# Gate logits as eight extra columns of the local attention's products, and expert rows in 68 tiles of 256 and 15 of 128 rows

## The chip, the cores and the metric

The kernel runs on one core of one Trainium2 chip, in one launch. The metric is the device time of one execution in microseconds (us), as the median of several runs. All arithmetic is in fp32, apart from a few bf16 constants.

## The reference

A batch of 16 images with 128 rows of text each becomes 16 sequences of 569 rows of 256 features. Three residual parts follow, and then a recurrent one. Cut to what matters here:

```python
h = concatenate([tokens(x), txt], axis=1)            # convolution and attention over 441 positions
h = h + attn(layernorm(h))                           # windows of 64 rows, 8 heads, out @ w_out.T + b_out
xf = layernorm(h).reshape(-1, 256)
logits = xf @ gate_w + gate_b                        # gate_w: 256 x 8
probs = softmax(logits)
top2_vals, top2_idx = top_k(probs, 2)                # two of the eight experts for each row
for e in range(8):                                   # 256 -> 512 -> 256, gelu between
    out += cw[:, e:e+1] * (gelu(xf @ w1[e] + b1[e]) @ w2[e] + b2[e])
h = h + out
h = h + layer1_attn(layernorm(h))                    # a cumulative sum over time
h = h + layer1_lstm(layernorm(h))                    # an LSTM over the 569 steps
```

The kernel runs an expert only on the rows that picked it. The logits of a row need the row after the attention's output projection and after its normalisation.

## The kernel before, in words

The rows are kept as 8 pairs of sequences (`NP`) with 9 chunks of 128 rows each (`NC`), 72 chunks in all. The work has three stages, one after the other.

**The first stage** makes the tokens, the window attention and the choice of experts. Several Python generators describe it: `features` and `projections` (convolution, queries and values), `tokens` (attention of the tokenizer), `norms` (the normalisation before the window attention), four copies of `windows` (one chunk each: `wtr` transposes, `wqk` queries and keys, `wsc` scores, `wv` values, `wpt` and `wav` the weighted sum, `wob` the output projection L777), `sent_rows` (the normalisation after it, into the tile `XN`), and `routing`. A planner, the class `Order`, replays the generators against a cost that each gives for its next instruction, and writes one fixed order of instructions for each engine. Every engine then works through its list in order. On GpSimd (POOL) the planner's `"POOL+"` and on VectorE (DVE) its `"DVE+"` steps are kept from running at the same time.

`routing` works on the nine chunks of a pair (the last pair in parts of 4, 3 and 2 chunks). For each group of up to four chunks it transposes the normalised rows (`rtr`, L800), copies them out of PSUM (`rxT`, L804), multiplies them by the gate's weights, padded to 32 columns so that four chunks lie side by side in the array (`lg`, L810), copies the result (`lgs`, L816), transposes it back (`lt`, L819) and adds the bias (L821). The softmax, the rank of each expert and the place of each row follow on DVE. `send` then scatters each chunk twice into the DRAM tensor `XS` with an indirect DMA from POOL (L908), so that the rows of one expert lie together.

**The second stage** runs the experts (`experts`). The rows of every expert are cut into tiles of 256 rows. Since each expert's last tile is only partly full, 79 tiles are provided for 18432 row places (2 experts for each of 9216 rows). A few small DVE instructions work out from the counts which expert and which first row each tile has (`need`, `where`, L1120 to L1149). SyncE (SP) reads these numbers into registers and issues for each tile the load of its expert's weights (`w`, 1154 KB, L1168) and of its rows (`xs`, L1174), into five buffers each. Four generators `tiles(slot)` take the tiles in turn. A tile is four transposes (`xtr`, L1212), eight products with the first weights (`hp`, L1241), four gelus on ScalarE (ACT, L1248), eight products with the second weights (`y`, L1255), a bias add on DVE (L1261), and two indirect DMAs back to the tensor `YT` (L1184). An fp32 product shows up as two records, each a weight load (PEld) and a pass (PE).

**The third stage** runs layer 1: `fronts`, `backs` and the LSTM's steps, in the order of a second planner.

Of the kernel before, what the change touches and what calls it, by code (L numbers as in the profile page):

```python
# [35 lines left out]
    ("bk1", 2), ("bq1", 2), ("bk2", 1), ("bq2", 1), ("ln_w", 2), ("ln_b", 2),  # L36
# [28 lines left out]
TILES = [(2 * 8 * 128 * len(g) + E * (TILE - 1)) // TILE for g in GROUPS]  # L65
# [229 lines left out]
def kernel(ctx: ExitStack, tc: tile.TileContext, a: dict, out: bass.AP):  # L295
# [63 lines left out]
    gw = route.tile([128, 2, 32], F32, name="gw")  # L359
# [16 lines left out]
    H, XN, made = {}, {}, []  # L376
# [12 lines left out]
    def rows_of(p, c):  # L389

        while len(made) >= ROWS:
            before = ("normed", *made[len(made) - ROWS])
            if before in first.events:
                break
            yield "at", before
        made.append((p, c))
        H[p, c] = hp.tile([128, D], F32, name=f"h{p}_{c}", tag="h", bufs=ROWS)
        return H[p, c]

    def texts():  # L400

        for p in range(NP):
            if p:
                yield "at", ("token", p - 1, 3)
            for c in (7, 6, 8):
                h = yield from rows_of(p, c)
                if c == 8:
                    yield "POOL", 0.3
                    nc.gpsimd.memset(h, 0.0)
                lo, hi, at = {6: (25, 64, 0), 7: (0, 64, 39), 8: (0, 25, 103)}[c]  # L410
                for s in range(2):
                    nc.sync.dma_start(
                        h[64 * s + lo : 64 * s + hi], a["txt"][2 * p + s][at : at + hi - lo, :]
                    )
            first.mark(("text", p), 8.0)

    def setup():
# [12 lines left out]
        nc.scalar.dma_start(wout, a["w_out"].rearrange("(k p) n -> p k n", p=128))  # L430
# [8 lines left out]
        nc.gpsimd.memset(gw, 0.0)  # L439
        nc.scalar.dma_start(gw[:, :, :E], a["gate_w"].rearrange("(k p) n -> p k n", p=128))  # L440
# [42 lines left out]
        for i, (name, w, b, to) in enumerate((("bv", wo, "bo", tok_b), ("vb", wout, "b_out", win_b))):  # L483
            v = tmp.tile([128, 2, 128], F32, name=f"{name}_every")
            for k in range(2):
                nc.vector.tensor_copy(v[:, k, :], col(name, k).to_broadcast([128, 128]))
            mm = place_of(f"{name}_row", 2 + i)
            for k in range(2):
                nc.tensor.matmul(mm[:, :D], v[:, k, :], w[:, k, :], start=(k == 0), stop=(k == 1))
            nc.vector.tensor_tensor(to, mm[:, :D], row(b), ALU.add)  # L490
# [77 lines left out]
    def tokens(slot):  # L568

        last = NIMG - 384  # L570
        for n in range(slot, 7 * NP, 2):
# [46 lines left out]
            for q, i in to:  # L618
                yield "DVE", 0.48
                nc.vector.scalar_tensor_tensor(  # L620
                    H[p, i][q], mm[q], share_[q], tok_b[q], ALU.mult, ALU.add
# [3 lines left out]
    def norm(h, to, name, slot):  # L625
# [3 lines left out]
        nc.vector.bn_stats(st, h)  # L629
# [4 lines left out]
        yield "POOL", 0.85  # L634
        nc.gpsimd.tensor_scalar(rstd, mv[:, 1:2], EPS, None, ALU.add)
        nc.gpsimd.tensor_tensor(rstd, rstd, mhalf[:, :1], ALU.pow)
        yield "DVE+", 0.5
        nc.vector.tensor_scalar(to, h, mv[:, 0:1], rstd, ALU.subtract, ALU.mult)
# [12 lines left out]
    def sent_rows(p, c, h, slot):  # L651

        if p not in XN:
            if p > 1:
                yield "at", ("sent", p - 2)
            if p not in XN:
                XN[p] = xnp.tile([128, NC, WIDE], F32, name=f"XN{p}", tag="XN", bufs=2)
                yield "POOL", 0.2
                nc.gpsimd.tensor_copy(XN[p][:, :, D], cols[:, COL["row"] + NC * p : COL["row"] + NC * (p + 1)])
        yield from norm(h, XN[p][:, c, :D], f"r{p}_{c}", slot)  # L660
# [11 lines left out]
    def windows(slot):  # L672

        kb, vb = KB[slot], VB[slot]
        for n in range(slot, NC * NP, WINDOWS):
# [28 lines left out]
            nc.gpsimd.tensor_tensor(h, h, win_b, ALU.add)  # L704
# [16 lines left out]
            v = place_of(f"wv{u}", slot)[:, :D].rearrange("p (w n) -> p w n", w=2)  # L721
            for w in range(2):
                for k in range(2):
                    yield "PE", 0.22, "64"
                    for odd in range(2):
# [4 lines left out]
                        )  # L730
            top = wk.tile([128, NH], F32, name=f"wtop{u}", tag=f"wtop{slot}", bufs=1)
            yield "DVE", 0.68
            nc.vector.tensor_reduce(top, S, AX.X, ALU.max)
            for odd in range(2):
# [39 lines left out]
            ob = place_of(f"wob{u}", slot)[:, :D]  # L774
            for m in range(2):
                yield "PE", D * COLUMN
                nc.tensor.matmul(ob, AT[:, m, :], wout[:, m, :], start=(m == 0), stop=(m == 1))  # L777
            yield "DVE", 0.42
            nc.vector.tensor_tensor(h, ob, h, ALU.add)
            nc.sync.dma_start(HD[p][:, c, :], h)  # L780
# [4 lines left out]
    def routing():  # L785

        for p, lo, hi in PARTS:
            u, n = f"{p}_{lo}", hi - lo
            pr = wk.tile([128, n, E], F32, name=f"pr{u}", tag="pr", bufs=1)
            for g0 in range(lo, hi, 4):  # L790
                m = min(4, hi - g0)
                xT = wk.tile([128, 2, 4, 128], F32, name=f"rxT{p}_{g0}", tag="rxT", bufs=1)
                for c0 in range(g0, g0 + m, 2):
                    two = min(2, hi - c0)
                    tr = place_of(f"rtr{p}_{c0}", 7).rearrange("p (k c n) -> p k c n", k=2, c=2)
                    for c in range(c0, c0 + two):
                        yield "at", ("normed", p, c)
                        for k in range(2):
                            yield "PE", TURN
                            nc.tensor.transpose(  # L800
                                tr[:, k, c - c0, :], XN[p][:, c, 128 * k : 128 * k + 128], ident
                            )
                    yield "ACT", 0.6
                    nc.scalar.copy(xT[:, :, c0 - g0 : c0 - g0 + two, :], tr[:, :, :two, :])  # L804

                lg = place_of(f"lg{p}_{g0}", 7)
                for k in range(2):
                    yield "PE", 0.24, "32"
                    for j in range(m):
                        nc.tensor.matmul(  # L810
                            lg[32 * j : 32 * j + 32, :128], gw[:, k, :], xT[:, k, j, :],
                            start=(k == 0), stop=(k == 1),
                        )
# [1262 lines left out]
```

## Time and profile before

The profiled execution took 3360.87 us itself; its span, in which the tables below are, is 3359.0 us.

| | |
|---|---|
| time before, median of 3 runs | 3378.91 us (3378.6 to 3380.3) |
| profiled execution, own time / span | 3360.87 / 3359.0 us |
| PE, weight loads, DVE, ACT, POOL busy | 3055.1, 2231.5, 2027.2, 1471.9, 786.6 us |
| mean granted TensorE clock | 0.978 |
| first stage, to the first expert product | 0 to 978 us |
| second stage, to the last `y` product's start | 978 to 1573 us |
| third stage | 1573 to 3359 us |

An engine's busy time is the union of its instructions' durations. A product's record is longer than its share of a sequence of products, since they are pipelined: what a product costs in a sequence is read as the length of the sequence divided by its number. A line of groups gives busy time and mean duration after the bar, and then the idle time of the engine just ahead of the group with what ended it.

### The profile page before, as it was taken

How to read it: one execution, taken by the hardware profiler on the slowest of the kernel's cores; microseconds unless marked ns; L12 is line 12 of the kernel's file. 1: busy time of each engine (PE TensorE's matmuls, PEld its weight loads, DVE VectorE, ACT ScalarE, POOL GpSimd, SP SyncE). 2: the span in 40 equal slices, each digit the busy share in tenths (PEclk: the TensorE clock that was granted, in tenths of full speed). 3: DMA queues.
4: the chain of work that ended last, by engine and by line, in shares of the span. 5: the costliest groups of instructions: out<-in, count | busy, mean ns of one | idle time of the engine just before them, and what ended most of it. 6: DMA issues, size and time to landing. Idle time of an engine off the chain costs nothing.

```text
span 3359.0 us, 134328 instructions
## 1 busy us (share of the span) xinstructions
PE 3055.1 (91%) x57536; PEld 2231.5 (66%) x57536; DVE 2027.2 (60%) x6787; ACT 1471.9 (44%) x5030; POOL 786.6 (23%) x1524
## 2 busy tenths in 40 slices
PE   5999999999859999997899999999999999999884
PEld 3666666666548888886566676766666666666652
DVE  4677777766732222222566777777777777766555
ACT  3545545454412222221444555555555555554442
POOL 1243554445533322232311001010101010100000
PEclk9999999999979999998999999999999999999997
DMA  5111221111176666664333333333333333333333
GB/s 180 53 46 57 89 79 54 55 38 41 42 251 234 220 231 225 225 229 141 100 100 88 90 82 86 84 94 78 97 77 92 84 93 79 76 91 80 90 103 113
DMA packets 276070, 366.81 MB, mean 109 GB/s; under 512 B 144480, under 2 KB 220176, under 8 KB 263312
## 3 DMA queue, kind: packets, MB, share of 16 engines
q1 hardware_dynamic: 249360, 300.91, 30.5%
q0 software_dynamic: 14496, 39.75, 3.1%
q10 hardware_dynamic: 11616, 17.56, 1.8%
q8 instruction: 451, 7.39, 0.9%
q14 instruction: 147, 1.20, 0.1%
HBM read 239.33 MB, written 118.75 MB: 107 GB/s over the span
## 4 chain that ended last, share of the span: by engine, by line
PE 37%; DVE 7%; ACT 5%; issue 2%; SPq 1%; DMA 1%; POOL 0%; ACTq 0%; DVEq 0%; POOLq 0%
PE gates L1741 13%; PE xm_False L1085 5%; PE out_gate L1750 2%; PE ek L1085 2%; PE po_False L1085 2%; PE z L1085 2%; PE v L1085 2%; PE eq L1085 2%; PE ds_False L1085 2%; ACT act L1762 1%; PE r_False L1085 1%; ACT th L1798 1%; DVE ab L1777 1%; DVE cT L1790 1%; DVE act L1783 1%
## 5 line engine op out<-in xcount | busy, mean ns | idle before, releaser
L1741 PE MATMUL gates<-W_hh,X 128*16 128x96 f32 (+1 forms) x18176 | 487.9, 248 | 63.9 <-DVE X L1805 61.6
L1741 PEld LDWEIGHTS gates<-W_hh,X 128*16 128x16 f32 (+1 forms) x18176 | 373.6, 103 | 258.5 <-DVE X L1805 245.0
L1248 ACT ACTIVATE hT<-hp,w 128x256 f32<-128x256 f32 x316 | 132.6, 472 | 481.5 <-PE hp L1241 314.5
L1762 ACT ACTIVATE act<-gates 128x96 f32<-128x96 f32 x568 | 142.1, 250 | 444.1 <-PE gates L1741 437.0
L1255 PE MATMUL y<-w,hT 128*128 128x256 f32 x1264 | 289.7, 382 | 5.2 <-ACT hT L1248 1.5
L1085 PE MATMUL xm_False<-W_ih,dxT_False 128*32 128x256 f32 x4352 | 292.3, 380 | 2.3 <-DVE dxT_False L1271 1.9
L1241 PE MATMUL hp<-xt,w 128*128 128x256 f32 x1264 | 287.6, 381 | 1.0 <-ACT hT L1248 1.0
L1777 DVE SCALAR_TENSOR_TENSOR ab<-act 128x64 f32<-128x64 f32 x568 | 127.9, 225 | 258.2 <-ACT act L1762 250.8
L1255 PEld LDWEIGHTS y<-w,hT 128*128 128x128 f32 x1264 | 236.8, 190 | 45.2 <-ACT hT L1248 14.4
L1684 PEld LDWEIGHTS <-nil 128*32 128x32 bf16 x4552 | 190.3, 94 | 111.0 <-issue 53.0
L1241 PEld LDWEIGHTS hp<-xt,w 128*128 128x128 f32 x1264 | 239.9, 191 | 35.7 <-ACT hT L1248 1.5
L1184 POOL DMA_INDIRECT YT<-ys,to x158 | 153.4, 971 | 440.4 <-DVE ys L1261 408.9
L1261 DVE TENSOR_TENSOR ys<-y,w 128x512 f32<-128x512 f32 x79 | 54.6, 691 | 316.3 <-PE y L1255 241.1
L1750 PE MATMUL out_gate<-W_hh,X 128*32 128x64 f32 x9088 | 233.8, 219 | 0.7 <-issue 0.7
L1690 ACT COPY gates<-xc 128x96 f32<-128x96 f32 x569 | 138.6, 244 | 182.0 <-DMA xc<-XCD 75.4
L1750 PEld LDWEIGHTS out_gate<-W_hh,X 128*32 128x32 f32 x9088 | 187.9, 110 | 2.9 <-issue 1.1
L1805 DVE SCALAR_TENSOR_TENSOR X<-toT,th 128x32 f32<-128x32 f32 x569 | 109.9, 193 | 120.5 <-ACT th L1798 116.9
L1798 ACT ACTIVATE th<-cT 128x32 f32<-128x32 f32 x569 | 130.5, 229 | 92.9 <-DVE cT L1790 43.1
L1301 POOL TENSOR_SCALAR d_False_rstd<-d_False_mv 128x2 f32<-128x2 f32 (+1 forms) x36 | 9.0, 250 | 671.8 <-DVE d_False_mv L1293 547.4
L908 POOL DMA_INDIRECT XS<-XN,at x144 | 149.1, 1035 | 45.6 <-issue 24.6
L693 PE MATMUL wqk<-wxT,wqkv 128*128 128x128 f32 x1152 | 150.6, 278 | 8.9 <-ACT wxT L687 8.6
L693 PEld LDWEIGHTS wqk<-wxT,wqkv 128*128 128x128 f32 x1152 | 139.4, 192 | 24.9 <-ACT wxT L687 13.5
(356 smaller groups left out, 6497.9 us busy)
## 6 DMA issues: line engine op xcount, KB each, us to landing
w<-in_wpack SPq DMA_DIRECT2D x79, 1154.0 KB
taps<-in_taps SPq DMA_DIRECT2D x16, 1764.0 KB
xc<-XCD SPq DMA_DIRECT2D x71, 384.0 KB
XCD<-xp_False SPq DMA_DIRECT2D x256, 96.0 KB
xs<-XS SPq DMA_DIRECT2D x79, 258.0 KB
yg<-YT SPq DMA_DIRECT2D x72, 256.0 KB
HD<-h SPq DMA_DIRECT2D x72, 128.0 KB
fh<-HD SPq DMA_DIRECT2D x72, 128.0 KB
```

What stands on the lines that cost most here:

```text
L693: nc.tensor.matmul(qk[:, j, m, :], wqkv[:, k, D * j + 128 * m : D * j + 128 * m + 128], xT[:, k, :], start=(k == 0), stop=(k == 1),)
L908: fill(0, nc.gpsimd.indirect_dma_start(out=XS[0], out_offset=bass.IndirectOffsetOnAxis(ap=at[:, i, c - lo : c - lo + 1], axis=0), in_=XN[p ...
L1085: nc.tensor.matmul(out[own], lhsT[:, own], rhs, start=start, stop=stop)
L1184: keep(nc.gpsimd.indirect_dma_start(out=YT, out_offset=bass.IndirectOffsetOnAxis(ap=to[:, i : i + 1], axis=0), in_=ys[:, i, :], in_offset= ...
L1241: nc.tensor.matmul(hp[:, i, :], w1[:, k, hc * 128 : (hc + 1) * 128], xT[:, k, :], start=(k == 0), stop=(k == 1),)
L1255: nc.tensor.matmul(y[:, i, :], hT[:, hc, 128 * i : 128 * i + 128], w2[:, hc, :], start=(hc == 0), stop=(hc == 3),)
L1684: nc.tensor.matmul(g[32 * q : 32 * q + 32, :n], nil[:, :32], nil[:, :n], start=True, stop=last)
L1741: nc.tensor.matmul(GC[32 * q : 32 * q + NB * (1 + half), :96], before[:, kk, NB * (1 - half) :], Whh[:, kk, own : own + 96], start=False, ...
L1750: nc.tensor.matmul(GO[32 * q : 32 * q + 32, :64], before[:, kk, :], Whh[:, kk, own : own + 64], start=False, stop=(kk == 1),)
L1762: nc.scalar.activation(act[:, :96], GC[:, :96], AF.Tanh, scale=0.5), begun.pop((k, t))
L1777: nc.vector.scalar_tensor_tensor(ab, act[:, :64].rearrange("p (g x) -> p g x", g=2), 1.0, act[:, 64:].rearrange("p (g x) -> p g x", g=2), ...
L1798: nc.scalar.activation(th.rearrange("p k x -> p (k x)"), cT, AF.Tanh, scale=0.5)
```

## The change

It has two parts, which share no instruction.

**Gate logits in the window attention.** Write g for `gate_w` with the mean of each column taken off (so that the normalisation's own subtraction of a mean has no effect on it). With h2 = h + attention, the logits are `rstd2 * (h2 @ g) + gate_b`. The setup makes g (`gate_sum`), W·g with W the output projection (`wout_t`, `wout_gate`) and the bias's part, and puts W·g as columns 256 to 263 of `wout`. The rows `h` get nine more columns: eight for h2 @ g and one for sqrt(var + eps) of the first normalisation, since the product takes `xT`, the normalised rows. In each chunk four small products (64 x 8) follow the value products, a DVE instruction scales them by that ninth column, the output projection is 264 columns wide, and after the second normalisation one DVE instruction multiplies by `rstd` and adds `gate_b`, into `LG`. POOL works out the ninth column with one more `pow`. The six steps in `routing` from `rtr` to the bias add fall away.

**Tiles of two sizes.** 68 tiles of 256 rows are taken from the full 256-row pieces of the experts, and what is left of each expert goes to 15 tiles of 128 rows. The tiles are worked through in the sequence 0 to 7, then a small one after every four large ones. A small tile loads half the rows and all of its expert's weights. More DVE instructions work out the places.

```diff
-TILES = [(2 * 8 * 128 * len(g) + E * (TILE - 1)) // TILE for g in GROUPS]
+WHOLE = [(2 * 8 * 128 * len(g) - E * TILE // 2 + TILE - 1) // TILE for g in GROUPS]
+TILES = [
+    w + (2 * 8 * 128 * len(g) + E * (TILE // 2 - 1)) // (TILE // 2) - 2 * w for w, g in zip(WHOLE, GROUPS)
+]
...
-    gw = route.tile([128, 2, 32], F32, name="gw")
+    gw = route.tile([128, 2, E], F32, name="gw")
...
-        H[p, c] = hp.tile([128, D], F32, name=f"h{p}_{c}", tag="h", bufs=ROWS)
+        H[p, c] = hp.tile([128, D + E + 1], F32, name=f"h{p}_{c}", tag="h", bufs=ROWS)
...
+        mm = place_of("gate_sum", 4)
+        for k in range(2):
+            nc.tensor.matmul(mm[:, :E], ones, gw[:, k, :], start=(k == 0), stop=(k == 1))
+        for k in range(2):
+            nc.vector.scalar_tensor_tensor(
+                gw[:, k, :], mm[:, :E], -1.0 / D, gw[:, k, :], ALU.mult, ALU.add
+            )
+        for m in range(2):
+            mm = place_of(f"wout_t{m}", 5)
+            woutT = tmp.tile([128, 2, 128], F32, name=f"woutT{m}")
+            for k in range(2):
+                nc.tensor.transpose(
+                    mm[:, 128 * k : 128 * k + 128], wout[:, m, 128 * k : 128 * k + 128], ident
+                )
+            nc.scalar.copy(woutT.rearrange("p k n -> p (k n)"), mm[:, :D])
+            mm = place_of(f"wout_gate{m}", 4)
+            for k in range(2):
+                nc.tensor.matmul(mm[:, :E], woutT[:, k, :], gw[:, k, :], start=(k == 0), stop=(k == 1))
+            nc.scalar.copy(wout[:, m, D:], mm[:, :E])
...
+        over = mv[:, 1:2]
+        nc.gpsimd.tensor_scalar(over, over, EPS, None, ALU.add)
+        nc.gpsimd.tensor_tensor(rstd, over, mhalf[:, :1], ALU.pow)
+        if name[0] == "w":
+            nc.gpsimd.tensor_tensor(h[:, D + E :], over, half, ALU.pow)
...
+        rstd = yield from norm(h, XN[p][:, c, :D], f"r{p}_{c}", slot)
+        yield "DVE", 0.19
+        nc.vector.scalar_tensor_tensor(
+            LG[p][:, c, :], h[:, D : D + E], rstd, frow("gate_b", E), ALU.mult, ALU.add
+        )
...
+            for k in range(2):
+                yield "PE", 0.06, "64"
+                for w in range(2):
+                    own = slice(64 * w, 64 * w + 64)
+                    nc.tensor.matmul(
+                        vg[own, D : D + E], xT[:, k, own], gw[:, k, :], start=(k == 0), stop=(k == 1)
+                    )
...
+            yield "DVE", 0.2
+            nc.vector.scalar_tensor_tensor(
+                h[:, D : D + E], vg[:, D : D + E], h[:, D + E :], win_b[:, D:], ALU.mult, ALU.add
+            )
...
-                yield "PE", D * COLUMN
+                yield "PE", (D + E) * COLUMN
                 nc.tensor.matmul(ob, AT[:, m, :], wout[:, m, :], start=(m == 0), stop=(m == 1))
...
-            for g0 in range(lo, hi, 4):
... 
+            for c in range(lo, hi):
+                yield "at", ("normed", p, c)
+            pr = LG[p][:, lo:hi, :]
...
+        each = (whole - 2 * slots) / (NT - whole)
+        order = sorted(
+            range(NT), key=lambda j: j if j < whole else 2 * slots - 0.5 + (j - whole) * each
+        )
...
-                            yield "PE", 256 * COLUMN
+                            yield "PE", 128 * n * COLUMN
                             nc.tensor.matmul(
-                                hp[:, i, :], w1[:, k, hc * 128 : (hc + 1) * 128], xT[:, k, :],
+                                hp[:, i, : 128 * n], w1[:, k, hc * 128 : (hc + 1) * 128], xT[:, k, :],
                                 start=(k == 0), stop=(k == 1),
                             )
...
-                for i in range(2):
+                for i in range(n):
                     for hc in range(4):
                         yield "PE", 256 * COLUMN
```

In a small tile `n` is 1, in a large one 2. The fixed order of PE and of ACT in the third stage is the same in both kernels; on DVE and SP a few of its instructions change places.

## The prediction

> **What bounds the kernel now.** I read the stages' table first (busy us of each engine in six stretches of the span; then the granted clock, the DMA share and GB/s):
>
> ```profile
> 34.00:100.00 66.00, 54.32 (x356) 32.80 (x357) 41.97 (x101) 31.20 (x84) 12.04 (x22) 0.94 0.32 116
> 100.00:880.00 780.00, 729.87 (x6460) 514.47 (x6458) 553.85 (x1458) 394.46 (x1073) 352.83 (x615) 1.00 0.16 56
> 880.00:978.00 98.00, 44.63 (x405) 33.95 (x404) 56.81 (x199) 25.01 (x64) 54.78 (x98) 0.74 0.50 170
> 978.00:1573.00 595.00, 587.46 (x2815) 509.01 (x2815) 141.14 (x484) 132.57 (x316) 180.75 (x331) 1.00 0.65 220
> 1573.00:3359.00 1786.00, 1628.15 (x47476) 1133.54 (x47474) 1228.18 (x4528) 885.58 (x3487) 178.77 (x432) 0.98 0.35 90
> ```
>
> The experts (978 to 1573) are PE's alone: 587 of 595 us. From 100 to 880 PE is busy 94%, with DVE second at 71%. From 880 to 978 no engine fills its time, which is a chain. The change leaves the last stage's order on PE alone; I count 0 there.
>
> The groups of the products that the change removes (busy us, mean ns):
>
> ```profile
> L800 PE MATMUL rtr<-ident,XN 128*128 128x128 f32 x144 | 26.3, 287 | 1.3 <-DVE part L887 0.6 <-DVE XN L638 0.5
> ...
> L810 PE MATMUL lg<-rxT,gw 128*32 128x128 f32 x288 | 15.7, 283 | 0.9 <-ACT rxT L804 0.7
> ...
> L819 PE MATMUL lt<-ident,lgs 128*128 128x128 f32 (+3 forms) x24 | 7.2, 301 | 1.9 <-ACT lgs L816 1.9
> ```
>
> Last the timeline (start, length), for rates and for the chain:
>
> ```profile
> 436.60 1.86 PEld L693 LDWEIGHTS wqk<-wxT,wqkv 128*128 128x128 f32 x16 [0.17 <-ACT wq L702]
> ...
> 907.83 0.38 PEld L810 LDWEIGHTS lg<-rxT,gw 128*32 128x32 f32 x16 [0.17 <-issue]
> ...
> 908.41 0.73 PEld L777 LDWEIGHTS wob<-wout,wAT 128*128 128x128 f32 x4 [0.20 <-ACT VB L737]
> ...
> 929.49 0.55 PEld L766 LDWEIGHTS wav<-wPT,VB 128*64 128x64 f32 x16 [0.20 <-ACT wPT L759]
> ...
> 940.08 0.71 PEld L800 LDWEIGHTS rtr<-ident,XN 128*128 128x128 f32 x4 [0.65 <-PE pos L876]
> ...
> 963.40 0.91 SPq L1168 DMA_DIRECT2D w<-in_wpack  x2
> ...
> 1203.02 3.42 PEld L1255 LDWEIGHTS y<-w,hT 128*128 128x128 f32 x16
> ```
>
> Here 16 passes of 256 columns take 3.42 us (0.214 each), 16 of 128 columns 1.86 (0.116), 16 of 64 by 64 with two side by side 0.55 (0.034). A gate group of four chunks holds PE from 907.83 to the next product at 908.41: 0.58 us. SP's loads of `w` in the steady experts stand at 1201.22 and, two tiles on, at 1216.28: **7.53 us for a tile**, and 79 x 7.53 = 595.
>
> [...]
>
> **The change, part by part.**
>
> *Tiles.* Eleven large tiles go: 11 x 7.53 = 82.8 us. A small one has 16 passes of 128 columns (16 x 0.116 = 1.86), 8 of 256 (1.71) and two transposes (the group L1212: 43.1 us for 316, 0.136 each, 0.27). A large tile by this sum is 32 x 0.214 + 4 x 0.136 = 7.39, measured 7.53, so I add 0.1 for its stalls: 3.94, times 15 = 59.1. Gain **23.7**. Bounds: with passes of exactly half (0.107) 26; with passes that keep the weight load's mean record of 0.191 a tile is 5.1 and the gain 6. I take the sequence's rate, since it is the same shape.
> Four more loads of 1154 KB cost nothing while PE covers them: a round of four large tiles and one small moves 5 x 1154 + 4.5 x 514 KB = 8.3 MB in 4 x 7.53 + 3.94 = 34 us, 243 GB/s; the steady stage shows up to 237, and the DMA-bound 950 to 1000 us 277. Without cover a small tile would last as long as its 1.45 MB: 5.2 us, 19 in all lost. SP issues two register reads and two DMAs more for each of four tiles; POOL sends seven scatters fewer (0.97 us each, idle there).
> The extra planning on DVE is 3 instructions ahead of the first tiles' numbers and 16 after them, some 0.18 us each, 3.4 in all: DVE ended at 957.1, and SP's first `w` at 963.40 waited for the last scatters, so 6.3 us of cover hides it. Without that it costs 3.4.
>
> *Gate path removed.* PE: 144 transposes at 0.116 = 16.7; 24 gate groups at 0.58 = 13.9[...]; 24 transposes back at 0.14 = 3.4[...]: **38** us. The busy sums (26.3 + 15.7 + 7.2 = 49) are the upper end. ACT loses the copies L804 (21.7) and L816 (6.4), DVE L821 (4.3): neither sets the pace.
> *Added.* 72 x 8 passes of 64 by 8[...], taken as wav's 34: 19.6[...]. Eight more columns on 288 passes: 8/256 of 0.214, 1.9. DVE gets two instructions per chunk: 72 x (0.2 + 0.19) = 28 us. POOL gets 72 `pow`: the row of the same form lasts 0.62, 45 us on an engine busy 353 of 780.
> So PE wins 38 - 21.5 = 16.5[...], and less than nothing only if DVE's part below decides. The new DVE step waits for the gate product and for POOL's `pow`; behind it on DVE stand the sums that PE's `wpt` needs. DVE's net 24 us are 3% of the stretch, and PE idles there 50 us, mostly for DVE: I give back 4. Gain **12.5**.
>
> *Setup.* Convolution starts at 33.97, right after the product `vb_row`, on which it waits. Now a chain stands ahead: DVE's two corrections (0.4), then twice a product pair (0.5 as L473) and an ACT copy (0.17), one 0.37 us copy, two more DVE copies (0.35), four more small passes (0.5). **Loss 3** (1 to 5); taps arrive earlier, so nothing hides it.
>
> *Tail.* From the last chunk's transposes (940.08) to its logits (L821, ended at 943.98) 3.9 us fall away, with the order on PE (after `pos`) that held them. What is late next is POOL: 18 scatters of 1.27 us are 22.9 of the 28.8 between 927.05 and 955.86, so at most 5.9 can go from there. In the new order POOL has the last chunk's subtraction behind five scatters, 6.4 us. Gain **4** (0 to 9).
>
> Sum: 23.7 + 12.5 - 3 + 4 = 37.2. The profiled execution then has a span of 3321.8 and 3323.7 of its own; it stood 18.0 under the median of the three runs, so against that I predict 3378.9 - 37 = **3342**.
>
> **Rivals.**
> *Only the experts pay.* The small products cost 53 ns, DVE takes back the rest, the tail stays with POOL: 16.5 - 11 - 5.5 = 0, so 23.7 - 3 = 21: 3358. For it: PE's idle time ends mostly on DVE. Against: PE is at 94%.
> *A small tile is not a small tile.* Its passes stay at the weight load's length or it waits for its weights: 6 + 12.5 - 3 + 4 = 19.5: 3359. For it: a small tile loads as many weights. Against: 0.116, and five buffers.
> *DVE becomes the bound of the first stage: slower.* From 100 to 880 it is at 71%, and at 80% in single stretches of 50 us. If each of 72 chunks pays both new instructions and their two waits (0.39 + 2 x 0.25 = 0.89 us, 64), PE's gain is void, since PE's in-order list waits: 23.7 - 3 - 64 + 4.3 + 4 = -35: 3414. It decides once a chunk's net delay passes some 0.35 us (25 over 72). Against: PE's own waits for DVE are only some 25 us in this stretch.
> *The whole gate path was on the path*[...]: 33 + 23.7 - 3 + 9 = 63: 3316.
>
> **How the numbers follow.** Chances: the forecast 0.58, only the experts 0.2, tile not small 0.06, the whole path 0.08, DVE 0.08. The forecast's own range is 3327 to 3354. With the two at 3358 and 3359 it reaches up to 3363; the low end, 3322, leaves out most of the 3316 case, the high end the DVE case. Within 0.2% is 6.8 us, about what this kernel's measurement can tell from no change. Faster than that takes all but the DVE case and a bit of the second and third failing together: 0.9; slower 0.06; the same 0.04.
>
> **What would show it.** In the new profile: first small-column passes behind `wv` at about 0.03 us each; the first stage's 100 to 880 work done some 12 us sooner; convolution starting near 37; the first expert product at about 964; the SP loads of `w` five to a round of 34 us, so the experts last 571; the last stage again 1786. A round above 36 us makes the tile part wrong; a first product after 975 makes the gate part wrong; DVE as the releaser of much more PE idle time makes the third rival right.

## The result, and the profile after

| | before | after |
|---|---|---|
| time, median of 5 runs each on one chip | 3378.91 us (3378.2 to 3382.1) | 3333.89 us (3330.9 to 3342.4) |
| ratio, 95% interval | | 0.9874 (0.9858 to 0.9889) |
| profiled execution, own time / span | 3360.87 / 3359.0 us | 3333.89 / 3332.1 us |
| mean granted TensorE clock | 0.978 | 0.973 |

The change saves 45.0 us between the medians, and 27 us between the two profiled executions: the one of before stood 18.0 us under its median, the one of after at its median. Most of what follows turns on these 18 us.

The stages' table of after (busy us of PE, PEld, DVE, ACT, POOL; granted clock, DMA share, GB/s), cut where the stages now begin:

```profile
36.20:100.00 63.80, 52.78 (x376) 33.11 (x378) 39.36 (x102) 31.55 (x85) 12.50 (x22) 0.95 0.33 120
100.00:880.00 780.00, 723.99 (x6592) 510.65 (x6588) 581.70 (x1579) 371.26 (x1012) 401.79 (x705) 0.99 0.17 58
880.00:976.00 96.00, 45.97 (x372) 36.84 (x373) 57.70 (x218) 22.53 (x59) 45.84 (x81) 0.67 0.43 144
976.00:1541.00 565.00, 558.07 (x2810) 491.04 (x2809) 143.47 (x508) 132.89 (x332) 174.10 (x316) 1.00 0.69 239
1541.00:3332.10 1791.10, 1631.48 (x47476) 1130.98 (x47474) 1229.21 (x4528) 885.76 (x3487) 179.67 (x434) 0.98 0.34 90
```

Against before's rows, the experts last 565 us in place of 595, the first expert product comes at 976 in place of 978, and the last stage, whose order on PE did not change, takes 1791 in place of 1786. Read so, the experts give 30 us, and everything done to the gate gives 2.

The experts' groups by form, SP's loads of `w` in the steady experts (start, length), and PE's sequence over one small tile:

```profile
L1309 PE MATMUL hp<-xt,w 128*128 128x256 f32 x1088 | 253.4, 382 | 0.0
L1309 PE MATMUL hp<-xt,w 128*128 128x128 f32 x240 | 31.6, 275 | 0.0
```

```profile
1201.81 0.33 SPq L1230 DMA_DIRECT2D w<-in_wpack  x1
...
1208.31 0.33 SPq L1230 DMA_DIRECT2D w<-in_wpack  x1
...
1211.96 0.33 SPq L1230 DMA_DIRECT2D w<-in_wpack  x1
...
1218.72 0.33 SPq L1230 DMA_DIRECT2D w<-in_wpack  x1
...
1228.65 0.33 SPq L1230 DMA_DIRECT2D w<-in_wpack  x1
...
1235.51 0.33 SPq L1230 DMA_DIRECT2D w<-in_wpack  x1
```

```profile
1207.29 2.35 PE L1309 MATMUL hp<-xt,w 128*128 128x128 f32 x14
1209.48 1.89 PE L1323 MATMUL y<-w,hT 128*128 128x256 f32 x8
```

Five loads, one round of four large tiles and one small, take 1235.51 - 1201.81 = 33.70 us. With a large tile at its 7.53, a small one adds 33.70 - 30.12 = **3.58 us**. From start to start its passes of 128 columns are 0.111 us apart over the whole stage, passes of 256 columns 0.216.

The new products of the first stage, by form, from 100 to 880, and for comparison the output projection of before:

```profile
L830 PE MATMUL wob<-wout,wAT 128*128 128x264 f32 x260 | 70.6, 399 | 0.0
L777 PE MATMUL wv<-gw,wxT 128*64 128x8 f32 x520 | 23.4, 195 | 0.0
```

```profile
L777 PE MATMUL wob<-wout,wAT 128*128 128x256 f32 x260 | 67.2, 385 | 0.5 <-ACT wAT L773 0.3
```

A small product's record is 195 ns, but they overlap: from the first of a chunk's eight records to the product behind them, 0.204 us pass in the median, 26 ns each. In products_twice (below), which issues them twice, the sixteen take 0.437 us, so the second eight add 29 ns each. The record of a `wob` pass has grown by 14 ns, but the passes stand only 7 ns further apart: 0.223 us from start to start, 0.216 before.

Setup and tail in the timeline of after, the setup first:

```profile
35.63 0.51 PE L518 MATMUL vb_row<-gw,ob_every 128*128 128x8 f32 x4
...
36.23 1.95 ACT L537 ACTIVATE fT<-taps,cols 128x220 f32<-128x220 f32 x4 [3.79 <-PE vb_row L518]
```

```profile
923.59 0.68 DVE L782 TENSOR_REDUCE wtop<-wS 128x8 f32<-128x512 f32 x1
...
927.13 2.13 PE L830 MATMUL wob<-wout,wAT 128*128 128x264 f32 x4 [0.67 <-issue]
...
929.46 1.05 POOL L794 TENSOR_TENSOR wS<-wS,wtop 128x512 f32<-128x512 f32 x1
...
939.26 0.43 DVE L832 TENSOR_TENSOR h<-wob,h 128x264 f32<-128x264 f32 x1 [3.91 <-PE wob L830]
...
948.81 0.17 DVE L920 CAST at<-slot 128x4 int32<-128x4 f32 x1 [0.20 <-issue]
```

and the same two places in before:

```profile
931.88 0.42 DVE L779 TENSOR_TENSOR h<-wob,h 128x256 f32<-128x256 f32 x1
...
950.66 0.17 DVE L901 CAST at<-slot 128x4 int32<-128x4 f32 x1 [0.20 <-DMA XS<-XN,at]
```

The convolution starts at 36.23, behind the new chain of small products. In the tail the last chunk's maxima are ready at 924.27 and its subtraction (L794) starts 5.2 us later, behind five scatters on POOL. The last sum `h` ends at 939.69 (932.30 before), and yet the last numbers for the scatters, `at`, are there at 948.98 (950.83 before): 9.3 us behind the sum in place of 18.5. How much of this is the shorter path to the logits, and how much the new order, is taken up under the tail's experiments.

### The profile page after: what moved, and what is told of

Its sections match the earlier page's. It is cut to its first block, busy times and chain, and to the rows that moved or that the text cites. A ratio compares the mean times of both kernels' runs of the same rounds, so it can differ in the third digit from the quotient of the medians.

```text
span 3332.1 us, 134813 instructions
## 1 busy us (share of the span) xinstructions
PE 3026.1 (91%) x57670; PEld 2213.9 (66%) x57670; DVE 2057.1 (62%) x6956; ACT 1448.2 (43%) x4986; POOL 821.3 (25%) x1581
## 4 chain that ended last, share of the span: by engine, by line
PE 38%; DVE 7%; ACT 5%; issue 2%; DMA 1%; SPq 1%; POOL 0%; ACTq 0%; DVEq 0%; POOLq 0%
PE gates L1811 13%; PE xm_False L1105 5%; PE out_gate L1820 2%; PE z L1105 2%; PE ek L1105 2%; PE v L1105 2%; PE po_False L1105 2%; PE ds_False L1105 2%; PE eq L1105 1%; PE r_False L1105 1%; ACT act L1832 1%; ACT th L1868 1%; DVE ab L1847 1%; DVE cT L1860 1%; DVE act L1853 1%
## 5 line engine op out<-in xcount | busy, mean ns | idle before, releaser
L1316 ACT ACTIVATE hT<-hp,w 128x256 f32<-128x256 f32 (+1 forms) x332 | 132.9, 453 | 450.2 <-PE hp L1309 343.4
L1323 PE MATMUL y<-w,hT 128*128 128x256 f32 x1208 | 276.3, 381 | 6.9 <-ACT hT L1316 6.5
L1309 PE MATMUL hp<-xt,w 128*128 128x256 f32 (+1 forms) x1328 | 277.7, 362 | 0.0
L1329 DVE TENSOR_TENSOR ys<-y,w 128x512 f32<-128x512 f32 (+1 forms) x83 | 53.4, 643 | 360.6 <-PE y L1323 315.8
L1309 PEld LDWEIGHTS hp<-xt,w 128*128 128x128 f32 x1328 | 234.8, 192 | 29.3
L1323 PEld LDWEIGHTS y<-w,hT 128*128 128x128 f32 x1208 | 226.3, 190 | 41.7 <-ACT hT L1316 11.2
L734 PEld LDWEIGHTS wqk<-wxT,wqkv 128*128 128x128 f32 x1152 | 140.5, 193 | 25.7 <-ACT wxT L728 16.0
```

What stands on the lines that cost most here:

```text
L734: nc.tensor.matmul(qk[:, j, m, :], wqkv[:, k, D * j + 128 * m : D * j + 128 * m + 128], xT[:, k, :], start=(k == 0), stop=(k == 1),)
L1309: nc.tensor.matmul(hp[:, i, : 128 * n], w1[:, k, hc * 128 : (hc + 1) * 128], xT[:, k, :], start=(k == 0), stop=(k == 1),)
L1323: nc.tensor.matmul(y[:, i, :], hT[:, hc, 128 * i : 128 * i + 128], w2[:, hc, :], start=(hc == 0), stop=(hc == 3),)
```

## The experiments

All were timed in turn with the kernel before on the same chip, over 3 or 5 rounds. Four chips were used for them, and before's median is 3381.4, 3378.0, 3368.6 and 3370.3 us on them, so only ratios, or kernels of one chip, are compared. Marks are in us from the start of the span of each profile: convolution's start, end of the last sum `h`, start of the first expert product, end of the last `y`. "Body" is from the first mark to the second, "tail" from the second to the third.

| kernel | chip | median | ratio to before (95%) | conv. | last `h` | first `hp` | last `y` | body | tail |
|---|---|---|---|---|---|---|---|---|---|
| before, profile on record | | 3378.9 | | 34.0 | 932.3 | 978.0 | 1576.3 | 898.3 | 45.7 |
| after | | 3333.9 | 0.9874 (0.9858 to 0.9889) | 36.2 | 939.7 | 976.0 | 1544.3 | 903.5 | 36.4 |
| before_again | A | 3380.9 | 1.0001 (0.9994 to 1.0008) | 32.8 | 954.0 | 995.9 | 1593.9 | 921.2 | 41.9 |
| tiles_only | A | 3348.8 | 0.9898 (0.9883 to 0.9913) | 32.7 | 951.2 | 994.6 | 1563.3 | 918.5 | 43.4 |
| gate_only | A | 3363.7 | 0.9950 (0.9936 to 0.9963) | 34.7 | 937.1 | 974.0 | 1571.9 | 902.4 | 36.9 |
| no_columns | A | 3328.8 | 0.9843 (0.9830 to 0.9857) | 35.7 | 938.1 | 975.5 | 1543.7 | 902.5 | 37.3 |
| products_twice | B | 3349.2 | 0.9908 (0.9894 to 0.9922) | 35.8 | 954.0 | 991.1 | 1558.6 | 918.2 | 37.1 |
| no_columns_held | B | 3313.8 | 0.9808 (0.9795 to 0.9821) | 36.2 | 926.1 | 963.8 | 1529.6 | 889.9 | 37.7 |
| before_no_gate | B | 3352.3 | 0.9922 (0.9906 to 0.9938) | 33.7 | 924.6 | 966.2 | 1562.0 | 890.9 | 41.6 |
| last_on_dve | B | 3333.0 | 0.9862 (0.9847 to 0.9876) | 35.2 | 938.1 | 975.5 | 1542.9 | 902.9 | 37.3 |
| kept_busy | C | 3329.4 | 0.9881 (0.9866 to 0.9896) | 35.0 | 923.5 | 961.0 | 1527.7 | 888.6 | 37.5 |
| products_alone | C | 3318.0 | 0.9854 (0.9839 to 0.9869) | 35.6 | 920.7 | 957.0 | 1522.9 | 885.1 | 36.4 |
| told_costs | C | 3340.7 | 0.9921 (0.9907 to 0.9935) | 35.7 | 940.9 | 983.7 | 1550.9 | 905.2 | 42.8 |
| root_by_product | D | 3326.7 | 0.9876 (0.9860 to 0.9892) | 35.8 | 925.9 | 963.7 | 1531.2 | 890.1 | 37.9 |

### The two parts, and before once more

**tiles_only** takes the diff's tile part alone, **gate_only** the rest of it alone. **before_again** has no edit.

> The kernel before with the two sizes of tiles alone; the gate path stays. Theory A (the tile part is all of the gain, about 29 us in the profile, because a small tile lasts 3.58 us and not 3.94): experts' stretch 566 us, span 28 to 31 us under the profile of before, median 27 to 32 us under before's. Theory B (the tile part is the 23.7 us of the forecast and the gate part brings the rest): 22 to 25 us. Theory C (tiles bring more than their stretch, since before's median stands 18 us over its own profile and after's does not): 40 to 46 us in the medians.

> The change without the small tiles: gate logits as columns, setup products and new tail, 79 tiles of 256 rows. Theory A: first expert product within 2 us of before (978), median within 3 us of before. Theory B (the forecast's 12.5 - 3 + 4): 13 us faster, first expert product at 964. Theory C: 15 to 18 us faster in the median, though the profile's first expert product stands at 976.

> The kernel before, unchanged, profiled a second time. If the 18 us between its first profile (3360.9) and its median (3378.9) is chance of that one execution, this profile has a time of 3375 to 3383 and shows where the 18 us are; if a profiled execution of this kernel is always that much shorter, it is 3358 to 3364 again.

The stages of before's second profile:

```profile
100.00:880.00 780.00, 723.96 (x6359) 508.36 (x6358) 540.65 (x1416) 388.99 (x1055) 348.07 (x607) 0.99 0.16 55
880.00:995.90 115.90, 61.58 (x514) 46.34 (x513) 71.55 (x241) 31.31 (x85) 60.15 (x107) 0.75 0.42 145
995.90:1590.90 595.00, 587.75 (x2816) 509.28 (x2816) 141.22 (x484) 132.59 (x316) 181.17 (x331) 1.00 0.65 220
1590.90:3383.50 1792.60, 1632.67 (x47475) 1136.60 (x47473) 1229.94 (x4528) 885.75 (x3487) 178.89 (x432) 0.98 0.35 90
```

The same program, in the same order on PE, reaches its first expert product at 995.9 where the profile on record has 978.0. From 100 to 880 it has got through 6359 matmul records, where the other had got through 6460. The experts are equal (595 us, 587.75 and 587.46 busy), and the last stage is 7 us longer. So the profile on record, at 3360.87 us, was an unusually short execution: none of the more than 50 timed runs of before shown here, on any chip, is under 3363. tiles_only, whose first stage is before's, agrees:

```profile
994.57 5.72 PE L1292 MATMUL hp<-xt,w 128*128 128x256 f32 x14
```

Against these two (chip A), gate_only's first expert product is 21.9 and 20.6 us sooner:

```profile
973.95 7.89 PE L1258 MATMUL hp<-xt,w 128*128 128x256 f32 x30
```

Of the 21.9, the setup takes back 1.9, the body gives 18.7 and the tail 5.0. The tiles alone save 32.6 us in the medians and 29.3 between first `hp` and last `y`; the gate alone saves 17.7. Theory A, that the gate gives nothing, was read from the short execution and fell. The two parts are additive within the intervals: 32.6 (29.4 to 39.6) and 17.7 (12.5 to 21.6) make 50 against 45.0, whose interval on 3378.9 is 37.5 to 48.

### The work that is removed and the work that is added, in a held order

Leaving work out lets the planner write another order. These kernels keep each `yield` with its cost and drop or double only the instruction, so that every other instruction keeps its place. Where the columns or the gate path are left out, the logits are the first eight entries of a row, so the rows go to other experts; the number of tiles stays, and so does the experts' time (565.8 us from first `hp` to last `y` in no_columns_held, 567.4 in last_on_dve).

**products_twice**:

```diff
-                    nc.tensor.matmul(vg[own, D : D + E], xT[:, k, own], gw[:, k, :], start=(k == 0), stop=(k == 1))
+                    for j in range(2):
+                        nc.tensor.matmul(vg[own, D : D + E], xT[:, j, own], gw[:, j, :], start=(j == 0), stop=(j == 1))
```

**no_columns_held** (and **no_columns**, where the yields went too):

```diff
-                    nc.tensor.matmul(vg[own, D : D + E], ...)
...
-            nc.vector.scalar_tensor_tensor(h[:, D : D + E], vg[:, D : D + E], h[:, D + E :], win_b[:, D:], ...)
...
-            ob = place_of(f"wob{u}", slot)[:, : D + E]
+            ob = place_of(f"wob{u}", slot)[:, :D]
...
-            nc.gpsimd.tensor_tensor(h[:, D + E :], over, half, ALU.pow)
...
-            LG[p][:, c, :], h[:, D : D + E], rstd, ...
+            LG[p][:, c, :], h[:, :E], rstd, ...
```

**before_no_gate**, an edit of the kernel before:

```diff
-                            nc.tensor.transpose(tr[:, k, c - c0, :], XN[p][:, c, ...], ident)
...
-                    nc.scalar.copy(xT[...], tr[:, :, :two, :])
...
-                        nc.tensor.matmul(lg[32 * j : 32 * j + 32, :128], gw[:, k, :], xT[:, k, j, :], ...)
...
-                nc.scalar.copy(lgs[: 32 * m], lg[: 32 * m, :128])
...
-                nc.tensor.transpose(lt, lgs[: 32 * m], ident[: 32 * m, : 32 * m])
...
-                    lt.rearrange("p (j e) -> p j e", e=32)[:, :, :E],
+                    XN[p][:, g0 : g0 + m, :E],
```

> The changed kernel with the eight small-column products behind each wv issued twice (the second set overwrites the first with the same numbers), every order held. In the changed kernel's trace 576 of them take 29 ns each, 17 us. Theory A (PE's amount of work is what the first stage is paced by): 15 to 17 us slower than the changed kernel, first expert product near 992. Theory B (chunks' chains and waits pace it; PE's work between two waits is partly hidden): 3 to 10 us slower.

> The changed kernel without its eight columns (the small products, eight columns of wob, the scaling on DVE and the third step on POOL are left out, logits from the first eight entries of each row), but with the order of every engine's list held as the changed kernel has it; the earlier run without columns had an order of its own. Theory A (work sets the pace): 15 to 20 us sooner at the first expert product than the changed kernel (976), 956 to 961. Theory B (chains and waits): 0 to 8 us sooner, with PE's idle time in 100 to 880 grown by what its work shrank.

> The kernel before with its gate path left out (no transposes of the normed rows, no gate products, no transposes back, no copies between them; logits from the first eight entries of each normed row) and nothing put in its place, the other instructions in the order of before. PE loses 31.3 us of passes from 100 to 880, 36 in all. Theory A (work sets the pace): first expert product 36 to 40 us sooner than in the second profile of before (996), at 956 to 960, and 37 us off the median. Theory B (chains and waits): 10 to 22 us sooner, 974 to 986.

> The changed kernel without the eight columns: the 64 x 8 products behind wv, the eight columns of wob, the scaling on DVE and the third step on POOL are left out, and the logits are made from the first eight entries of each row in place of the gate's product (so the rows go to other experts; the number of tiles is the same). If the added work is what eats PE's saving (16.5 us forecast, 15.3 + 4.5 us of added PE time in the trace), the first stage ends 15 to 20 us sooner than in the changed kernel: first expert product 956 to 961. If the first stage is paced by something else than PE's amount of work (the order of its in-order list, waits for ACT and DVE, the clock), it ends within 5 us of the changed kernel: 971 to 976.

The first expert product of products_twice and of no_columns_held:

```profile
991.13 8.33 PE L1310 MATMUL hp<-xt,w 128*128 128x256 f32 x30
```

```profile
963.80 6.67 PE L1299 MATMUL hp<-xt,w 128*128 128x256 f32 x30
```

All of chip B stand beside last_on_dve (below), which is within 2 us of after in every mark. Doubling 17 us of small products costs 15.3 us of body and 16.1 in the median: nearly one for one, so **PE's amount of work does pace the first stage**. Leaving all the columns' work out gains 13.0 in the body and 19.3 in the median. The two differ because the two profiles are 21.6 us apart, of which 8.3 lie behind the last `y`, where the edit doesn't reach. Leaving before's gate path out gains 27.7 to 30.3 in the body (against tiles_only and before_again, of chip A; against the short profile on record only 7.4) and 25.7 in the median on its own chip; its 36 us of PE passes were worth some 0.7 to 0.8 us each.

By the bodies, 29 removed and 13 added make 16 us, where gate_only's body is 16.1 to 18.7 shorter, so the sum closes. By the medians it does not close as well: 25.7 removed and 19.3 added make 6.4; with the setup's loss of some 2 and the tail's gain of some 5 beyond before_no_gate's that is 9, where gate_only's median gains 17.7. The medians' intervals are some 5 us to either side, and the bodies of one order differ by 15 us and more from profile to profile (last section). So what the new order as such contributes is not settled: nothing by the one account, some 9 us by the other.

no_columns alone would have been read the other way, as if the columns cost nothing: with an order of its own it has a first expert product at 975.5 like after's, 12 us later than no_columns_held, though it does the same work. Its chip was another, but the ratios to before say the same (0.9843 and 0.9808, and their intervals do not meet).

### What an order is worth

**told_costs** changes two numbers that only the planner sees:

```diff
-                yield "PE", 0.06, "64"
+                yield "PE", 0.118, "64"
-                yield "PE", (D + E) * COLUMN
+                yield "PE", 0.244
```

> The changed kernel with the planner told the measured lengths of the added PE work (0.118 us for four small products in place of 0.06, 0.244 us for a 264-column pass in place of 0.446); nothing else. The order that comes out is another one. Two orders of the same work have differed by 12 us at the first expert product (the two runs without columns: 975.5 and 963.8). If the order is worth that much here too: 8 to 15 us either way; if those two were an exception: within 4 us of the changed kernel.

It is 11.3 us slower than kept_busy on its chip (whose ratio, 0.9881, is after's within the interval, below), its body 16.6 us longer, its tail 5.3 us. So the same work in another order is worse by two thirds of what the gate part brings. It does not show that better costs make a worse order: the first new number is near the measured one (four records of 26 to 29 ns), but a `wob` product is two passes of 0.223 us, 0.445 in all, which is what the planner was told before (0.446), and the 0.244 of this run is about half of that. The expectation took one pass for the whole product. Why this order is worse was not followed up.

### DVE's and POOL's part of the columns

**products_alone** makes only that part of no_columns_held's edit that is on DVE and POOL (the scaling, the power, the eight columns of the sum); PE's products stay. **root_by_product**:

```diff
-            nc.gpsimd.tensor_tensor(h[:, D + E :], over, half, ALU.pow)
+            nc.gpsimd.tensor_tensor(h[:, D + E :], over, rstd, ALU.mult)
```

> The changed kernel with PE's part of the columns kept (the small products, 264 columns of wob) but the scaling on DVE, the third step on POOL and eight columns of the sum left out (logits from the first eight entries), orders held. If PE's part is the cost (products twice: +15.1 at the first expert product): first expert product within 3 us of the changed kernel, 973 to 976. If DVE's and POOL's part and their waits are most of it (the third rival): 964 to 968, near the run without columns.

> The changed kernel with the third step on POOL (a power, 0.59 us) replaced by a product of the two numbers that it already has, (var + eps) times its inverse root, orders held. POOL's other short steps with one factor last 0.24 to 0.27, so POOL's work shrinks by 72 x 0.33 = 24 us. The run with only PE's part of the columns (no such step, no scaling on DVE) was 11 us faster than the kept-busy run on its chip. If POOL's step is what cost that: 5 to 11 us faster than the changed kernel (ratio 0.984 to 0.986). If it was DVE's scaling and its wait, or the spread between executions of one order (10 us in the first stage): within 4 us of the changed kernel (ratio 0.986 to 0.989).

POOL's group in after and in root_by_product, from 100 to 880:

```profile
L671 POOL TENSOR_TENSOR h<-w_mv,half 128x1 f32<-128x1 f32 x65 | 38.5, 592 | 0.0
```

```profile
L671 POOL TENSOR_TENSOR h<-w_mv,w_rstd 128x1 f32<-128x1 f32 x67 | 13.9, 207 | 5.3
```

The product takes 207 ns where the power took 592, 28 us less on POOL over 72 chunks, and the ratio stays at 0.9876 against 0.9874: POOL's `pow` costs nothing that these intervals (some 5 us) can tell. products_alone is 11.4 us faster than kept_busy in the median, 3.5 in the body. The expectation's 964 to 968 or 973 to 976 can't be used for it, since the same instructions as after's stand at 961.0 on that chip. Of the 10.7 us between the two profiles, 5.9 lie behind the last `y`, where the edit doesn't reach. What DVE's scaling and its wait cost is somewhere from 3 to 11 us, and by this nearer to 3; it is not settled closer.

### The tail

**last_on_dve** moves one subtraction, **kept_busy** adds products that nobody reads (12 behind the last chunk's `wsc`, as shown, 4 behind each of the last two `wpt`, 12 and 40 behind their `wob`, 160 behind the last `pos`):

```diff
-            nc.gpsimd.tensor_tensor(S, S, top..., ALU.subtract)
+            last = (p, c) == (NP - 1, NC - 1)
+            (nc.vector if last else nc.gpsimd).tensor_tensor(S, S, top..., ALU.subtract)
```

```diff
+            keep_busy(12, p == NP - 1 and c == 8)
...
```

> The changed kernel with the last chunk's subtraction of the row maxima on DVE, not on POOL, where it stood 5.2 us behind five scatters (ready at 924.27, started at 929.46). If that queue is what cost the tail, the last chunk's sum h ends at 933 to 935 (939.7 in the changed kernel) and the first expert product stands at 970 to 972 (976.0): 4 to 6 us faster. If the scatters behind it then end last (POOL), less than 2 us.

> The changed kernel with products that nobody reads put into PE's gaps at the end of the first stage (12 behind the last chunk's scores, 4 behind each of the last two chunks' transposes, 12 and 40 behind their last products, 160 behind the last count), orders held. In the changed kernel the granted clock is half from 919.6 to 981.1 and the last chunks' products take twice as long (wob 2.13 us for four records, 1.16 before that). If the clock is what costs the tail: full clock again in most of 925 to 970, last sum h 3 to 5 us sooner after the last wqk, first expert product at 968 to 972, 5 to 8 us faster in all. If chains on DVE and POOL set the tail, the clock recovers and the end moves by less than 2 us.

last_on_dve in the timeline:

```profile
925.40 2.13 PE L833 MATMUL wob<-wout,wAT 128*128 128x264 f32 x4 [0.67 <-issue]
...
927.57 0.43 DVE L835 TENSOR_TENSOR h<-wob,h 128x264 f32<-128x264 f32 x1 [2.99 <-PE wob L833]
...
928.18 0.68 DVE L795 TENSOR_TENSOR wS<-wS,wtop 128x512 f32<-128x512 f32 x1
```

The maxima were ready at 922.55, and the subtraction still starts 5.6 us later: on DVE it stands behind the sum of the chunk before, which waits for `wob`. One queue took the other's place, and the tail stayed (37.3 us). kept_busy beside after, from 880 to shortly before the first expert transposes:

```profile
880.00:955.00 75.00, 54.93 (x512) 48.35 (x506) 44.50 (x178) 16.59 (x44) 33.91 (x60) 0.92 0.46 144
```

```profile
880.00:970.00 90.00, 42.31 (x356) 33.55 (x356) 54.91 (x207) 22.53 (x59) 45.84 (x81) 0.68 0.39 126
```

The filler products lift the granted clock from 0.68 to 0.92, and the tail stays again (37.5 us; ratio 0.9881). So PE's half clock behind the last sum went with its idling here (PE busy 42.31 of 90 us at 0.68, 54.93 of 75 at 0.92), and costs next to nothing. For the last chunks' own products this isn't shown: the clock was at half from 918.5 to 925.3 in kept_busy too, and its last `wob` took 2.13 us as in after.

What shortened the tail can be read from before_no_gate, which has no transposes and no gate products either, but before's order:

```profile
924.17 0.42 DVE L779 TENSOR_TENSOR h<-wob,h 128x256 f32<-128x256 f32 x1 [1.35 <-issue]
...
931.47 0.17 DVE L805 TENSOR_TENSOR pr<-XN,flow 128x16 f32<-128x16 f32 x1
...
938.33 0.17 DVE L885 CAST at<-slot 128x4 int32<-128x4 f32 x1 [0.20 <-issue]
```

From the last sum's end to `at` it takes 13.9 us, where before_again and tiles_only take 15.9 (the profile on record 18.5) and after 9.3, and its tail stays at 41.6 us. Leaving the path out in before's order is thus worth some 2 us; the last logits (L805) still stand on DVE behind the ranking of the three chunks before them. In after the last logits (L699, 941.70) come 2 us behind the sum. So the larger part of the tail's gain comes with the new order.

## Why the prediction was right, step by step

The forecast was 3342 us, 37.2 off before; measured were 45.0 off, with 37.5 to 48 in the interval. The direction, both main mechanisms and their order of size were right. The terms:

- **Tiles, 23.7: too small, 29.8 measured** (between first `hp` and last `y`: 598.1 in before_again, 598.3 in the profile on record, 568.3 in after). The failing step is "3.94". A small tile adds 3.58 to a round, so 82.8 - 15 x 3.58 = 29.1. The passes take 0.111 and not 0.116, the transposes 0.109 from start to start where the 0.136 came from a group's busy time, and the 0.1 added "for its stalls" isn't there. By these spacings a small tile's own passes sum to 3.72 (16 x 0.111, 8 x 0.216, 2 x 0.109); by an estimate from the last 0.14, the four large tiles of a round take a little under 7.53 each, so they stall less beside a small one. DMA covers the extra weights, at 239 GB/s against the 243 worked out.
- **The rival with a tile that isn't small** is out: 275 ns for the record, 111 from start to start. The weight loads' own records, here in after from 100 to 1545, are 190 and 193 ns for 128 columns, whether passes of 256 columns (`y`) or of 128 (`wqk`) follow, and 138 for 64:

```profile
L1323 PEld LDWEIGHTS y<-w,hT 128*128 128x128 f32 x1208 | 226.3, 190 | 41.7 <-ACT hT L1316 11.2 <-issue 0.6
...
L734 PEld LDWEIGHTS wqk<-wxT,wqkv 128*128 128x128 f32 x1088 | 132.7, 193 | 23.6 <-ACT wxT L728 14.3 <-issue 7.5
...
L768 PEld LDWEIGHTS wv<-wqkv,wxT 128*64 128x64 f32 x1100 | 62.4, 138 | 25.2 <-DVE wS L758 18.7 <-issue 2.6 <-DVE picked L880 0.3
```

The loads overlap the passes, and a pass is not held to their 190 ns: halving the moving columns halved it (0.216 to 0.111). Two small products side by side start 7 ns apart, and 26 is the mean.
- **Two more rivals** are out by gate_only's 17.7: "only the experts pay", with 53 ns for a small product (from 16 weight loads of `wv` in 0.85 us in before) where 26 to 29 were measured, leaves the gate nothing but the setup's loss, and "the whole gate path was on the path" gives it 33 - 3 + 9 = 39, of which the 33 was the author's estimate.
- **Gate path removed, 38: too large.** Of it 34 are the products and gate groups (16.7, 13.9 and 3.4); the last 4, for gaps around the 24 transposes back, was the author's estimate, and before shows 1.9 us of idle PE ahead of them in all. Left out alone it is worth 28 to 30 in the body, 26 in the median: on a stage that PE fills to 93%, a us of PE work was worth 0.7 to 0.8 when it was taken away. **Added, 21.5 and 4 given back: too large too.** The small products cost 26 to 29 ns each (15 to 17 us, not 19.6), the wider `wob` 7 ns on 288 passes (2.0, forecast 1.9), and all of it together 13 in the body, 19 in the medians. Both terms are too large, so the errors cancel in part, and that the net came near is in part luck: 16 to 19 in the body, forecast 12.5.
- **Setup, loss 3**: 1.9 to 3.4 measured. **Tail, gain 4**: 5 to 6.5. The reason given, the 3.9 us of the logits' path, is a smaller part of it: left out in before's order the path is worth 2, and the rest came with the new order. The step "what is late next is POOL" named five scatters ahead of the last subtraction, and these did come, but DVE's list held it as long in last_on_dve.
- **DVE as the bound**: out. The waits of PE in after, from 100 to 880, with the total, the number and the longest:

```profile
PE wav L819 <- ACT wPT L812: 8.5, 14, 1.0
PE wpt L807 <- DVE wS L803: 6.9, 11, 1.2
PE wv L768 <- DVE wS L758: 5.5, 13, 0.8
```

and in before's profile on record:

```profile
PE wpt L754 <- DVE wS L750: 8.0, 7, 2.5
PE wv L726 <- DVE wS L717: 6.9, 8, 1.9
PE wqk L693 <- ACT wxT L687: 6.2, 11, 1.4
```

PE's waits for DVE did not grow; all of them together are 21.8 us in after and 26.3 in before. What grew is the wait for ACT's copy `wPT`, by some 6 us (2.8 before); why was not followed up.

- **The 18.0 us** is the step that came out right for a reason it didn't have. The forecast was a difference, 37.2, taken from one profile and set off from the median, as if the profile stood 18 under it in all its kinds of work. Between the two profiles of before, 24.5 us apart, 17.9 lie ahead of the first expert product, where the gate part works, and 7 in the last stage; none lie in the experts. Against usual executions the gate gives its 17.7 us; against this one it seems to give 2. That a difference worked out from so short an execution also held for the median is luck, as far as the prediction goes.
- **The signs** failed where they were absolute times. "A first product after 975 makes the gate part wrong": it came at 976.0, and the gate part was right. The same sequence of instructions has it at 961 to 964 on chips C and D. The experts' 571 us came out at 565, by the tile's term. The signs that held were lengths within one stretch: a round of 34 us (33.7), small products at 0.03 us (0.026), a setup that ends near 37 (36.2).

## What to carry to other kernels

Before a difference is worked out from a profile, see how far that execution stands from the median and in which stage; a second profile of the same kernel costs less than a wrong attribution, and signs should be lengths of a round or a path, not times since the start. Where a planner writes the order, test a piece of work by leaving out its instruction and keeping its place: two orders of the same work differed by 11 to 12 us here, nearly as much as the piece of work in question. A tile of half the rows is priced from start to start of its own passes in a sequence of that shape, and a stall isn't added on unless the sequence shows one.

## What the runs showed of the hardware

One fixed order of instructions took from 888.6 to 903.5 us in the body (kept_busy, root_by_product, last_on_dve and after, which are alike there but for POOL's step and the last chunks), and before's from 898.3 to 921.2. The two short ones, kept_busy and root_by_product, ran on chips C and D, where before's median is 8 to 9 us lower than on B too, so a part of this can be the chip. Where after and root_by_product part by the largest step, some 5 us, the clock differs:

```profile
570.00:600.00 30.00, 25.93 (x220) 18.63 (x220) 14.94 (x39) 12.96 (x37) 18.10 (x31) 0.89 0.38 132
```

```profile
565.00:595.00 30.00, 28.08 (x279) 21.31 (x278) 19.48 (x46) 15.59 (x43) 17.89 (x32) 1.00 0.38 131
```

The first is after's, with 6.8 us of half clock, the second root_by_product's, with none. In the records of the clock of after and of before's profile on record, such stretches last 3.41, 6.83, 13.65, 20.48, 47.79 and 61.44 us, all multiples of 3.41; only the last of each, some 42 us, is not, and it runs past the end of the span. Before's two profiles have one of them from 100 to 880 (6.8 us, a mean granted clock of 1.00), and four (17 us in all, 0.99). Why one kernel meets them differently from run to run was not shown. By an estimate from these lengths, half clock for 10.2 us more costs at most half of that, 5.1, and in this stretch the chunks' last sums of the two profiles part by 15 us; so most of it is something else, or what follows from the clock in the waits. So it is with after and root_by_product: they part by 11 us there, with 10.2 and 3.4 us of half clock, worth at most 3.4. The rest wasn't settled.
